# A graph network's head on one core: edge-list work moved in between the rows of the first table

## The chip, the core and the metric

The kernel runs on one core of a Trainium2 chip. The core has TensorE (PE in the profile; PEld is its weight load), VectorE (DVE), ScalarE (ACT), GpSimd (POOL) and SyncE (SP), which share an on-chip memory, SBUF, of 128 partitions; the large tables lie in the chip's DRAM and are moved by DMA. The metric is device time in microseconds, median of several runs.

## What is computed

Two layers on a graph of 12,500 nodes with 128 features and 212,500 edges, sorted by target node; an edge has a source, a target and one of nine types. Each layer normalises the rows, adds up the sources' rows for every target, and puts the sums through small dense layers:

```python
h = jnp.maximum(_layernorm(x, axis=-1), 0.0)
x = x + _L0_gnn_ref(h, edge_index, edge_type_9, 12500, ...)   # sum over edges of h[src] @ W_msg.T + emb[type], then a GRU cell
h = jnp.maximum(_layernorm(x, axis=-1), 0.0)
x = x + _L1_gnn_ref(h, edge_index, ...)                       # (1 + eps) * h + sum over edges, dense, batch norm, relu, dense
```

with `jax.ops.segment_sum(msg, dst, num_segments=num_nodes)` as the sum over edges in layer 0.

## The kernel before

**The head** (first 124 us of the profile) makes what layer 0 reads. It has two strands that share nothing but the engines.

The rows: x comes in 25 slices of up to 512 nodes (4 tiles of 128 rows). For each slice `normed` takes mean and variance on DVE (L426, L427), the root on ACT (L428), its reciprocal and the offset on DVE (L429, L430), and writes relu of the normalised rows on ACT (L434). `split0` cuts the fp32 rows into three bf16 parts, so that their sum is nearly exact: a cast on POOL (L444), a subtraction on DVE (L445), a cast (L446) and a subtraction (L447) on POOL. SP stores the three parts as rows of `table0` in DRAM (L208). `rows_ahead` has four buffers for the relu's result `h` and the three parts `hp0`. Eight slices of x are loaded at the start (L276), the others as their buffers come free.

The edge list: dst, src and type arrive as 128 by 1664 integers by nine DMAs issued on ACT (L268 to L273). DVE turns them into floats (L791, L793), adds nine to the type of an edge to itself (L796, L797), and packs the three into a word each (L814 to L817), which SP stores as `packed` (L818). PE and ACT turn dst, src and type into chunks of 128 edges (L806, L807). To find where each of 28 groups of 252 target nodes begins, DVE compares every 16th dst with the 28 group leads at once (L826) and adds up (L830); a matmul with ones sums over the partitions (L845), and `row_edge` (L853) says from which edge each row of the sort starts. L869 to L881 count the edges in front of the groups and look for lists that the fast way can't hold. The weights are loaded and turned by `first_weights` and what follows it (L411 to L416), with DMAs issued on POOL.

In the program's text the order is: lists' DMAs, x loads, constants, weights, list work, rows, checks of the lists. A planner orders each engine's instructions: of those whose inputs are there by its reckoning, the one that stands first in the text goes first. So it can fill gaps with later work. Each engine then runs its queue in order.

**The sort and the chunks.** From `in_order` (L1420) on, four engines keep the order of the text. One loop goes over 1064 chunks of 128 edges: for each chunk POOL gathers 128 rows of `table0` (L1218), DVE writes a 0/1 matrix of edge against node for eight chunks at a time (`m`, L1226), and PE multiplies (L1239, L1242). After each chunk the loop takes one step of `make_buckets`, which sorts the edges of the 28 groups by block of source nodes: it fetches the packed words with `row_edge` (L910), takes them apart on DVE (L948 to L971), then compares and swaps (L476) and turns (L599, L605). It also takes one step of `loading`, which puts `table0` into the SBUF table `held` in 24 DMAs (L1336, L1339); `held`'s end is cleared first (L1333). When the sort is through, this order ends, and the rest of layer 0 runs groups and chunks side by side under the planner again. Layer 1 repeats the scheme on the new rows.

**Memory.** Tiles that are no longer needed give their place to later ones, and the first instruction to touch a later tile waits for whoever used that place last. The head's tiles (`edges`, `xs`, `rows_ahead`) lie where later `cell`, `keys`, `matches0`, `held` and `buckets` lie.

Of the kernel before, what the change touches and what calls it, by code (L numbers as in the profile page):

```python
# [38 lines left out]
F32 = mybir.dt.float32  # L39
BF16 = mybir.dt.bfloat16  # L40
F32R = mybir.dt.float32r
I32 = mybir.dt.int32
AF = mybir.ActivationFunctionType
OP = mybir.AluOpType
AX = mybir.AxisListType
# [6 lines left out]
P = 128  # L52
SLICE = 512
BATCH = 8
BLOCK = 256
GROUP = 252
# [21 lines left out]
def tile_gnn(  # L78
# [175 lines left out]
    nodes0 = lists0.tile([P, QJ, QI, GROUPS - FIRST], BF16, name="nodes0")  # L254
    codes0 = lists0.tile([P, QJ, QI, GROUPS - FIRST], BF16, name="codes0")
# [9 lines left out]
    for name, v, pad in (("dst", dst, N), ("src", src, N), ("typ", edge_type, 0)):  # L265
        t = as_is[name] = epool.tile([P, ET, P], I32, name=f"{name}_is")
        nc.gpsimd.memset(t[:, full_t, :], pad)
        nc.scalar.dma_start(t[:, :full_t, :],  # L268
                            v[:full_t * P * P].rearrange("(t r e) -> r t e", r=P, e=P))
        r0 = full_t * P * P  # L270
        nc.scalar.dma_start(t[:rest_r, full_t, :],
                            v[r0:r0 + rest_r * P].rearrange("(r e) -> r e", e=P))
        nc.scalar.dma_start(t[rest_r:rest_r + 1, full_t, :rest_e],  # L273
                            v[r0 + rest_r * P:E].rearrange("(r e) -> r e", r=1))
    xpool = edges.enter_context(tc.tile_pool(name="xs", bufs=8))
    xs_of = {s: load_x(slices[s], xpool) for s in range(8)}  # L276
# [130 lines left out]
    def first_weights_done():  # L407
# [3 lines left out]
    first_weights(pool0)  # L411
    w_t = transposed((("1", w1), ("2", w2)), weights)
    b1_t, gamma_t, beta_t = (column(weights, v, n) for v, n in
                             ((b1, "b1_t"), (gamma, "gamma_t"), (beta, "beta_t")))
    b2_t = spread(weights, b2, P, "b2_t")
    eps1 = spread(weights, eps, P, "eps1")  # L416

# [20 lines left out]
    def split0(h, sl, cast, engine):  # L438

        m, p = len(sl.tiles), sl.high  # L440
        hp = env.rows.tile([P, PER, W0], BF16, name="hp0")
        part = [hp[:p, :m, k * D:(k + 1) * D] for k in range(PARTS0)]
        h = h[:p, :m, :]
        cast(part[0], h)  # L444
        nc.vector.tensor_tensor(h, h, part[0], op=OP.subtract)  # L445
        cast(part[1], h)  # L446
        engine.tensor_tensor(part[2], h, part[1], op=OP.subtract)  # L447
        return hp
# [339 lines left out]
    as_f = {}  # L788
    for name in ("dst", "src"):
        t = as_f[name] = epool.tile([P, ET, P], F32, name=f"{name}_f")  # L790
        nc.vector.tensor_copy(t, as_is[name])  # L791
    typ_f = as_f["typ"] = epool.tile([P, ET, P], F32, name="typ_f")
    nc.vector.tensor_scalar(typ_f, as_is["typ"], 0.0, float(NTYPES - 1), op0=OP.max, op1=OP.min)  # L793
    nc.vector.tensor_copy(as_is["typ"], typ_f)
    to_self = epool.tile([P, ET, P], F32, name="to_self")
    nc.vector.tensor_tensor(to_self, as_f["dst"], as_f["src"], op=OP.is_equal)  # L796
    nc.vector.scalar_tensor_tensor(typ_f, to_self, float(NTYPES), typ_f, op0=OP.mult, op1=OP.add)  # L797
    for b in range(0, ET, 4):
        k = min(4, ET - b)
        for name, t in (("dst", nodes), ("src", idx0), ("typ", code0)):  # L800
            some = min(k * P, t.shape[1] - b * P)
            if some <= 0:
                continue
            ps = turnp.tile([P, 4, P], F32, name="work")
            for j in range(some // P):
                nc.tensor.transpose(ps[:, j, :], as_f[name][:, b + j, :], ident)  # L806
            nc.scalar.copy(t[:, b * P:b * P + some], ps.rearrange("p k r -> p (k r)")[:, :some])  # L807
    to_f = epool.tile([P, cols0], F32, name="to_f")
    nc.vector.tensor_tensor(to_f, nodes[:, :cols0], start0, op=OP.subtract)
    nc.vector.tensor_scalar(to0, to_f, -1.0, float(BLOCK - 1), op0=OP.max, op1=OP.min)  # L810


    word = as_is["src"]
    nc.vector.tensor_single_scalar(word, word, 18, op=OP.logical_shift_left)  # L814
    nc.vector.tensor_single_scalar(as_is["dst"], as_is["dst"], 4, op=OP.logical_shift_left)
    nc.vector.tensor_tensor(word, word, as_is["dst"], op=OP.bitwise_or)
    nc.vector.tensor_tensor(word, word, as_is["typ"], op=OP.bitwise_or)  # L817
    nc.sync.dma_start(packed[:ET * P * P].rearrange("(t r e) -> r t e", r=P, e=P), word)  # L818
    tail = epool.tile([P, GE // P], I32, name="tail")
    nc.vector.memset(tail, N << 4)  # L820
    nc.sync.dma_start(packed[ET * P * P:].rearrange("(p c) -> p c", p=P), tail)

    samples = ET * P // SAMPLE
    leads = iota(epool, [P, GROUPS], [[GROUP, GROUPS]], base=SPLIT, name="leads")
    before = epool.tile([P, GROUPS, samples], BF16, name="before")
    nc.vector.tensor_tensor(  # L826
        before, as_f["dst"].rearrange("p t e -> p (t e)")[:, None, ::SAMPLE].to_broadcast([P, GROUPS, samples]),
        leads[:, :, None].to_broadcast([P, GROUPS, samples]), op=OP.is_lt)
    sampled = epool.tile([P, GROUPS], F32, name="sampled")
    nc.vector.tensor_reduce(sampled, before, axis=AX.X, op=OP.add)  # L830
    spread_sampled = epool.tile([P, 2, P], F32, name="spread_sampled")
    nc.vector.memset(spread_sampled, 0.0)
    for h in range(2):
        nc.vector.tensor_copy(spread_sampled[:, h, :GP].rearrange("p (g r) -> p g r", r=GROUP_ROWS),
                              sampled[:, :, None].to_broadcast([P, GROUPS, GROUP_ROWS]))
        nc.vector.tensor_copy(spread_sampled[:, h, GP:GP + GROUPS // 2], sampled[:, h::2])

    ps = turnp.tile([P, 4, P], F32, name="work")  # L840
    row_edge = lists0.tile([P, 2], I32, name="row_edge")
    first_edge = epool.tile([P, 2], F32, name="first_edge")
    in_group = epool.tile([P, 2], F32, name="in_group")
    for h in range(2):
        nc.tensor.matmul(ps[:, 0, h:h + 1], spread_sampled[:, h, :], ones, start=True, stop=True)  # L845

        here = in_group[:, h:h + 1]
        nc.vector.tensor_scalar(here, part_row[:, 0:1], float(-HALF), float(GROUP_ROWS * HALF - h * REST),
                                op0=OP.mult, op1=OP.add)
        nc.vector.scalar_tensor_tensor(here, here, behind, here, op0=OP.mult, op1=OP.subtract)  # L850
        nc.vector.tensor_scalar(here, here, float(GROUP_ROWS * HALF), None, op0=OP.add)
    nc.vector.tensor_scalar(first_edge, ps[:, 0, 0:2], -1.0, 0.0, op0=OP.add, op1=OP.max)
    nc.vector.scalar_tensor_tensor(row_edge, first_edge, float(SAMPLE), in_group, op0=OP.mult, op1=OP.add)  # L853

    layer_rows, env.rows = env.rows, edges.enter_context(tc.tile_pool(name="rows_ahead", bufs=4))
    for s, sl in enumerate(slices):
        xs = xs_of[s] if s in xs_of else load_x(sl, xpool)
        hp = split0(normed(sl, xs), sl, nc.gpsimd.tensor_copy, nc.gpsimd)
        rows_dma(table0, hp, sl, True)
    env.rows = layer_rows  # L860
    first_weights_done()
    nc.vector.tensor_scalar(eps1, eps1, 1.0, None, op0=OP.add)


    sent = epool.tile([P, 1], F32, name="sent")
    hit = epool.tile([P, ET * P], BF16, name="hit")
    bound = epool.tile([P, 1], F32, name="bound")
    nc.vector.memset(bound, 0.5 - SPLIT)
    nc.scalar.activation(hit, nodes, AF.Sign, bias=bound, accum_out=sent)  # L869
    totals = lists0.tile([1, 1], F32, name="totals")  # L870
    column_sums(totals, sent, -0.5, ET * P * P / 2)

    ends = stat.tile([P, 3], F32, name="ends")
    nc.vector.tensor_reduce(ends[:, 0:1], to_f[:, :CH0], axis=AX.X, op=OP.min)
    nc.vector.scalar_tensor_tensor(to_f, nodes[:, :cols0], float(SPLIT0), to_f, op0=OP.is_lt, op1=OP.mult)
    nc.vector.tensor_reduce(ends[:, 1:2], to_f[:, :CH0], axis=AX.X, op=OP.max)
    nc.vector.tensor_reduce(ends[:, 2:3], nodes[:, CH0:ALL], axis=AX.X, op=OP.min)
    nc.vector.tensor_scalar(ends[:, 0:1], ends[:, 0:1], -1.0, None, op0=OP.mult)
    nc.vector.tensor_scalar(ends[:, 1:2], ends[:, 1:2], float(1 - first_chunks.window), None, op0=OP.add)
    nc.vector.tensor_scalar(ends[:, 2:3], ends[:, 2:3], -1.0, float(SPLIT0), op0=OP.mult, op1=OP.add)  # L880
    worst_of(excess[:, 0:1], ends)  # L881
# [923 lines left out]
```

## Time and profile before

| | us |
|---|---|
| median of 3 runs (2593.80 to 2598.58) | 2594.92 |
| the profiled execution, all | 2603.78 |
| its span, first to last instruction | 2602.0 |
| head: to the first instruction of the sort on DVE (L948) | 124.02 |
| first gather of the table's rows on POOL (L1218) | 123.36 |
| busy in the span: PE, DVE, POOL, ACT | 2250.3, 2117.8, 1860.4, 1322.5 |
| busy from 0 to 124 us: PE, DVE, ACT, POOL | 13.73, 102.70, 57.19, 81.13 |

A line of a profile's group reads: line of the kernel, engine, operation, output<-input by the program's names, shape and type, number of instructions | busy us in all, mean ns of one | idle us of the engine just ahead of them, and what ended that idle time. A line of the timeline reads: start, length (of a merged run of the same instruction), engine, line, operation, names, number, and in brackets the idle time ahead of it with its releaser.

### The profile page before, as it was taken

To read this page: it belongs to the slowest core of one execution; us is meant where nothing else is said; L and a number is where in the kernel's file an instruction comes from. 1 tells how busy PE (TensorE), PEld (TensorE's weight loads), DVE (VectorE), ACT (ScalarE), POOL (GpSimd) and SP (SyncE) were. 2 spreads that over 40 slices of the span, in tenths; PEclk is the share of its full clock that TensorE was granted. 3 is DMA by queue.
4 is the path that set the end of the run, shared out by engine and by line. 5 is a ranking of instruction groups with operands and counts; after the bars stand their busy time and mean duration, and the time that the engine had idled before them with its cause. 6 is when DMAs were issued, how large, how long until landed. Compare 5 with 4: busy or idle time off the path is not lost. (4 is left out here: it accounts for less than half of the span.)

```text
span 2602.0 us, 52858 instructions
## 1 busy us (share of the span) xinstructions
PE 2250.3 (86%) x19810; PEld 1896.3 (73%) x19834; DVE 2117.8 (81%) x3899; ACT 1322.5 (51%) x2726; POOL 1860.4 (71%) x1886
## 2 busy tenths in 40 slices
PE   2033469899999999999999797899999999999996
PEld 1023347677677777777777575799999999999995
DVE  8898759896568878788787565699999999999983
ACT  4475125455566655656565364444444444444443
POOL 4876477777777777777777676377777777777770
PEclk9996659999999999999999898899999999999998
DMA  5662234454445444545455356655555555555584
GB/s 155 203 205 67 84 100 128 122 128 127 131 132 143 131 134 127 149 129 132 127 150 131 90 144 187 171 154 156 157 158 159 159 159 156 159 160 160 153 217 128
DMA packets 308267, 374.73 MB, mean 144 GB/s; under 512 B 44815, under 2 KB 263093, under 8 KB 308001
## 3 DMA queue, kind: packets, MB, share of 16 engines
q0 software_dynamic: 85504, 197.27, 28.7%
q1 hardware_dynamic: 217451, 171.44, 23.3%
q8 instruction: 158, 2.59, 0.4%
q10 hardware_dynamic: 5046, 2.55, 0.3%
q14 instruction: 108, 0.88, 0.1%
HBM read 327.18 MB, written 43.91 MB: 143 GB/s over the span
## 5 line engine op out<-in xcount | busy, mean ns | idle before, releaser
L1218 POOL DMA_INDIRECT g<-table,idx x1064 | 1070.9, 1006 | 354.9 <-issue 298.4
L1218 POOL DMA_INDIRECT g<-front,idx x690 | 692.8, 1004 | 258.5 <-issue 189.5
L1239 PE MATMUL bank<-m,g 128*128 128x128 bf16 (+25 forms) x5790 | 687.8, 232 | 101.5 <-DMA g<-table,idx 53.0
L1379 ACT CAST rows<-bank 128x384 bf16<-128x384 f32 x936 | 441.8, 478 | 410.3 <-PE bank L1377 407.6
L1542 ACT CAST rows<-bank 128x512 fp32r<-128x512 f32 x686 | 402.7, 588 | 470.8 <-PE bank L1539 468.3
L1539 PE MATMUL bank<-mine,take 126*128 126x256 f32 x2744 | 475.0, 295 | 16.0 <-issue 11.6
L1377 PE MATMUL bank<-held,take 128*128 128x384 bf16 x1872 | 464.5, 328 | 2.4 <-ACT rows L1379 1.6
L1386 PE MATMUL bank<-put,rows 128*128 128x252 bf16 x2808 | 460.1, 272 | 0.0
L1239 PEld LDWEIGHTS <-g 128*128 128x128 bf16 x3912 | 299.5, 103 | 200.0 <-DMA g<-table,idx 94.5
L1552 PE MATMUL bank<-put,rows 128*128 128x256 f32 x2744 | 443.1, 284 | 2.2 <-DVE put L1527 1.9
L1527 DVE TENSOR_TENSOR put<-places,nodes 128x1024 fp32r<-128x1024 f32 x343 | 412.9, 1213 | 5.4 <-PE bank L1552 5.4
L1358 DVE TENSOR_TENSOR put<-places,nodes 128x1008 bf16<-128x1008 f32 x234 | 281.3, 1202 | 157.0 <-PE bank L1388 156.7
L1539 PEld LDWEIGHTS bank<-mine,take 126*128 126x128 f32 x2744 | 374.2, 191 | 28.0 <-issue 21.8
L1552 PEld LDWEIGHTS bank<-put,rows 128*128 128x128 f32 x2744 | 378.0, 190 | 6.8 <-issue 3.6
L1386 PEld LDWEIGHTS <-rows 128*128 128x128 bf16 x2808 | 274.9, 98 | 130.1 <-issue 4.1
L1522 DVE TENSOR_SCALAR take<-others,own_row 126x512 fp32r<-126x512 bf16 x686 | 302.4, 491 | 64.1 <-PE bank L1539 33.6
L1226 DVE TENSOR_TENSOR m<-places,to 128x1024 bf16<-128x1024 f32 (+1 forms) x220 | 312.4, 1420 | 20.3 <-PE bank L1242 11.9
L476 DVE TENSOR_TENSOR key<-key 128x512 f32<-128x512 f32 (+1 forms) x470 | 297.2, 666 | 12.0 <-ACT key L607 4.0
L1239 PEld LDWEIGHTS bank<-m,g 128*128 128x128 f32 x1878 | 270.9, 190 | 2.7 <-DMA g<-front,idx 1.6
L1242 PE MATMUL bank<-m,kindsc 128*128 128x128 bf16 (+2 forms) x1304 | 269.9, 218 | 0.0
L1388 PE MATMUL bank<-put,kindsb 128*128 128x252 bf16 x936 | 254.4, 272 | 0.0
L1369 DVE TENSOR_SCALAR take<-others,own_row 128x512 bf16<-128x512 bf16 x468 | 151.6, 360 | 38.9 <-PE bank L1377 38.4
(329 smaller groups left out, 2189.7 us busy)
## 6 DMA issues: line engine op xcount, KB each, us to landing
others<-sources SPq DMA_DIRECT2D x343, 126.0 KB
others<-sources SPq DMA_DIRECT2D x234, 128.0 KB
g<-table,idx POOLq DMA_INDIRECT x1064
g<-front,idx POOLq DMA_INDIRECT x690
xs<-in_x_dram SPq DMA_DIRECT2D x39, 256.0 KB
table<-hp SPq DMA_DIRECT2D x24, 384.0 KB
held<-table SPq DMA_DIRECT2D x24, 384.0 KB
mine<-back SPq DMA_DIRECT2D x28, 252.0 KB
```

Of the source, the lines that this page charges most:

```text
L476: nc.vector.tensor_tensor(o, a, b, op=op)
L1218: nc.gpsimd.indirect_dma_start(out=into if table is table0 else into.bitcast(F32), out_offset=None, in_=table, in_offset=bass.IndirectOffs ...
L1226: nc.vector.tensor_tensor(m[:, :n, :], places[:, None, :w].to_broadcast([P, n, w]), to[:, c0:c0 + n, None].to_broadcast([P, n, w]), op=OP. ...
L1239: nc.tensor.matmul(tiles[0][:, lo:hi], g[:, j * D:(j + 1) * D], mk, start=False, stop=final and j == parts - 1, skip_group_check=True)
L1377: nc.tensor.matmul(ps, take[:, t, :], held[:, t0 + t, :], start=t == 0, stop=t == 1)
L1379: nc.scalar.copy(rows_, ps)
L1386: nc.tensor.matmul(sums[:, :GROUP], rows_[:, j * D:(j + 1) * D], put, start=False, stop=final and j == PARTS0 - 1, skip_group_check=True)
L1522: nc.vector.tensor_scalar(take[:GT, t, :n * P], others[:GT, :n * P], own_row[:GT, t:t + 1], None, op0=OP.is_equal)
L1527: nc.vector.tensor_tensor(put[:, :n, :], places[:, None, :].to_broadcast([P, n, BLOCK]), nodes1[:, j, q:q + n, None].to_broadcast([P, n, B ...
L1539: nc.tensor.matmul(ps[:, k, :], take[:GT, t, :], mine[bucket[1]][:GT, t, :], start=t == 0, stop=t == 1)
L1542: nc.scalar.copy(rows_, ps)
L1552: nc.tensor.matmul(to[:, c:c + BLOCK], rows_[:, k, j * D:(j + 1) * D], put, start=False, stop=final and j == PARTS - 1, skip_group_check=True)
```

## The change

The list's nine DMAs are issued on SP, between the loads of the first eight slices of x. The list work becomes a generator, `listed_edges`, of which each slice of rows but the first takes two steps, so that it stands between the slices in the text. The group leads are no longer compared in one instruction on DVE: ACT takes 28 Sign passes over every 16th dst, each with its sum. `split0` makes its first cast on ACT. The words of the sort are fetched in the head, into the place that the sort's result (`nodes0`, `codes0`, now one tile) takes later. The weights' loading moves behind the fifth slice. `rows_ahead` has six buffers. `held`'s end is cleared after its 24 loads.

```diff
-    nodes0 = lists0.tile([P, QJ, QI, GROUPS - FIRST], BF16, name="nodes0")
-    codes0 = lists0.tile([P, QJ, QI, GROUPS - FIRST], BF16, name="codes0")
+    both0 = lists0.tile([P, 2, QJ * QI * (GROUPS - FIRST)], BF16, name="both0")
+    nodes0, codes0 = (both0[:, k, :].rearrange("p (j i g) -> p j i g", j=QJ, i=QI) for k in range(2))
+    raw0 = both0.bitcast(I32).rearrange("p k n -> p (k n)")[:, :HALF]
...
-        nc.scalar.dma_start(t[:, :full_t, :],
+        nc.sync.dma_start(t[:, :full_t, :],
...
-    xs_of = {s: load_x(slices[s], xpool) for s in range(8)}
+    xs_of = {}
+    for s in range(8):
+        xs_of[s] = load_x(slices[s], xpool)
+        if s in (1, 3, 5):
+            load_edges(*(("dst", dst, N), ("src", src, N), ("typ", edge_type, 0))[s // 2])
...
-        cast(part[0], h)
+        nc.scalar.copy(part[0], h)
         nc.vector.tensor_tensor(h, h, part[0], op=OP.subtract)
-        cast(part[1], h)
-        engine.tensor_tensor(part[2], h, part[1], op=OP.subtract)
+        nc.gpsimd.tensor_copy(part[1], h)
+        nc.gpsimd.tensor_tensor(part[2], h, part[1], op=OP.subtract)
...
+    def listed_edges():
...
+        leads = iota(epool, [P, GROUPS], [[-GROUP, GROUPS]], base=-SPLIT, name="leads")
+        nc.vector.tensor_scalar(leads, leads, 0.5, None, op0=OP.add)
+        signs = epool.tile([P, samples], BF16, name="signs")
+        for g in range(GROUPS):
+            nc.scalar.activation(signs, as_f["dst"].rearrange("p t e -> p (t e)")[:, ::SAMPLE], AF.Sign,
+                                 bias=leads[:, g:g + 1], accum_out=sampled[:, g:g + 1])
+            if g % 4 == 3:
+                yield
...
-    before = epool.tile([P, GROUPS, samples], BF16, name="before")
-    nc.vector.tensor_tensor(
-        before, as_f["dst"].rearrange("p t e -> p (t e)")[:, None, ::SAMPLE].to_broadcast([P, GROUPS, samples]),
-        leads[:, :, None].to_broadcast([P, GROUPS, samples]), op=OP.is_lt)
-    sampled = epool.tile([P, GROUPS], F32, name="sampled")
-    nc.vector.tensor_reduce(sampled, before, axis=AX.X, op=OP.add)
...
+        for h in range(2):
+            nc.gpsimd.indirect_dma_start(
+                out=raw0[:, h * REST:(h + 1) * REST], out_offset=None,
+                in_=packed.rearrange("(e one) -> e one", one=1),
+                in_offset=bass.IndirectOffsetOnAxis(ap=row_edge[:, h:h + 1], axis=0))
...
-    layer_rows, env.rows = env.rows, edges.enter_context(tc.tile_pool(name="rows_ahead", bufs=4))
+    listed_ = listed_edges()
+    layer_rows, env.rows = env.rows, edges.enter_context(tc.tile_pool(name="rows_ahead", bufs=6))
     for s, sl in enumerate(slices):
         xs = xs_of[s] if s in xs_of else load_x(sl, xpool)
-        hp = split0(normed(sl, xs), sl, nc.gpsimd.tensor_copy, nc.gpsimd)
+        hp = split0(normed(sl, xs), sl)
         rows_dma(table0, hp, sl, True)
+        for _ in range(2 if s else 0):
+            next(listed_, None)
+        if s == 4:
+            first_weights(pool0)
...
+    for _ in listed_:
+        pass
...
     def make_buckets(keys, pool, psum):
-        raw = keys.tile([P, HALF], I32, name="key")
-        for h in range(2):
-            nc.gpsimd.indirect_dma_start(
...
-        nc.vector.memset(held[:, full:, :], 0.0)
-
         def loading():
-            nc.sync.dma_start(held[:N - full * P, full, :], table0[full * P:N, :])
             for t in range(0, full, 4):
...
                 yield
+            nc.vector.memset(held[:, full:, :], 0.0)
+            nc.sync.dma_start(held[:N - full * P, full, :], table0[full * P:N, :])
```

The steps of `listed_edges` that are not shown are the old instructions in this order: casts of dst and src, the Sign passes, the type, the packing and its store, `row_edge`, the fetch of the words, the edges to themselves, the turned chunks, the checks.

## The prediction

> **What bounds the kernel now.** I read the page's slices first: the first two (130 us) are the only ones in which TensorE (PE) is nearly idle while VectorE (DVE) works, and the diff moves instructions there alone. So I cut that head into stages with the view of busy time by window, then read its groups of instructions, then its end in the timeline. By window (columns: stretch, length, busy us and count for PE, PEld, DVE, ACT, POOL, granted clock, DMA share, GB/s):
>
> ```profile
> core 0: us, PE busy (x) PEld busy (x) DVE busy (x) ACT busy (x) POOL busy (x), PEclk, DMA share, GB/s
> 0.00:4.50 4.50, 0.00 (x0) 0.00 (x0) 1.13 (x8) 0.00 (x0) 3.94 (x14) 1.00 0.48 143
> 4.50:20.00 15.50, 1.11 (x4) 0.71 (x4) 11.09 (x64) 1.78 (x4) 8.66 (x13) 1.00 1.07 293
> 20.00:43.00 23.00, 11.90 (x40) 7.29 (x40) 21.07 (x21) 11.29 (x27) 2.90 (x5) 1.00 0.15 45
> 43.00:119.20 76.20, 0.71 (x4) 0.26 (x4) 69.18 (x278) 44.11 (x121) 61.73 (x77) 1.00 0.65 190
> 119.20:124.00 4.80, 0.00 (x0) 0.00 (x0) 0.22 (x1) 0.00 (x0) 3.90 (x6) 1.00 0.67 182
> ```
>
> Four stages follow one another: loading (DMA full, ScalarE (ACT) empty), the edge lists (DVE full, POOL and DMA empty), the rows of the table (DVE 69.18 of 76.2, 91%; POOL 81%; ACT 58%), and 4.8 us in which DVE does nothing. DVE is the fullest throughout: 102.5 us busy of 119.2. The groups of 0 to 119.2 us, shapes kept apart (busy, mean ns | idle before):
>
> ```profile
> L434 ACT ACTIVATE h<-xs,nb,rs 128x128 f32<-128x128 f32 x98 | 39.1, 480 | 17.3 <-DVE nb L430 15.8 <-issue 0.9 <-DMA table<-hp 0.5
> L447 POOL TENSOR_TENSOR hp<-h,hp 128x512 bf16<-128x512 f32 x24 | 28.7, 1196 | 0.9
> L445 DVE TENSOR_TENSOR h<-h,hp 128x512 f32<-128x512 f32 x24 | 27.5, 1150 | 6.6 <-POOL hp L444 6.1
> ...
> L446 POOL CAST hp<-h 128x512 bf16<-128x512 f32 x24 | 16.3, 680 | 11.3 <-DVE h L445 8.3 <-DVE nb L430 3.1
> L444 POOL CAST hp<-h 128x512 bf16<-128x512 f32 x24 | 16.0, 670 | 19.7 <-ACT h L434 19.7
> ...
> L430 DVE SCALAR_TENSOR_TENSOR nb<-mv,rs 128x4 f32<-128x4 f32 x24 | 6.7, 294 | 0.0
> ...
> L826 DVE TENSOR_TENSOR before<-dst_f,leads 128x2912 bf16<-128x2912 f32 x1 | 5.1, 5067 | 0.0
> ...
> L830 DVE TENSOR_REDUCE sampled<-before 128x28 f32<-128x2912 bf16 x1 | 3.2, 3167 | 0.0
> ```
>
> L444 first starts at 45 us (its 19.7 us of idle): no row of the table is made earlier, because ACT's first instruction comes at 18.2 us, behind its nine DMA issues, and DVE then does the lists first. The timeline at the head's end:
>
> ```profile
> 118.98 0.17 DVE L934 MEMSET front<- 128x128 f32 x1
> ...
> 120.61 1.04 POOL L910 DMA_INDIRECT key<-packed,row_edge  x1 [0.16 <-issue]
> ...
> 122.88 0.22 DVE L1333 MEMSET held<- 128x192 uint32 x1 [3.74 <-DMA table<-hp]
> ...
> 123.36 0.95 POOL L1218 DMA_INDIRECT g<-table,idx  x1 [0.44 <-issue]
> ...
> 124.02 0.54 DVE L948 TENSOR_SCALAR ints<-key 128x512 int32<-128x512 int32 x1 [0.92 <-DMA key<-packed,row_edge]
> ```
>
> DVE waits 3.74 us in a memset for the last stores of the table and 0.92 us for the keys; only then does the sort (L948 on) begin. From there DVE sets the pace: in each 10 us from 140 to 220 it is busy 9.7 to 9.8, 16 compares (10.59 us) and one match per eight chunks, and PE waits for the match (3.93 us at 172, 5.29 at 184). Gathers have slack: PE is done with the first eight chunks at 138.7 us, and DVE needs their match buffer at 147.27. So what counts is when L948 starts: 124.0 now, with 2478.0 us behind it.
>
> **The change, part by part.** *DVE.* The comparison with all group leads and its reduction go: 5.07 + 3.17 = 8.24 us. Two small scalings come: some 0.15 us each by L310's row. 102.5 - 8.2 + 0.3 = 94.6 us. Inside that lies waiting that counts as busy: L445 takes 0.69 us where POOL runs nothing and 1.63 where it runs L447, on average 1.150; L430 takes 0.14 or up to 1.11, on average 0.294. That is 24 x 0.46 + 24 x 0.154 = 14.7 us blocked by POOL. Per slice POOL's 0.67 + 0.68 + 1.20 = 2.55 us lose the first cast: 26% less. I take 26% of 14.7, 3.9 us, off: 90.7 us. Bounds: half of it goes (87.3), or none goes and a dozen list operations, which had POOL idle beside them, each meet half a 1.2 us L447 (101.8).
>
> *ACT.* Off go nine DMA issues, which hold it until 18.2 us. On come 25 casts of 128x512 and 28 Sign passes over 104 samples. A cast costs 0.586 (L807, same size, from PSUM): 24.5 x 0.586 = 14.4 us. A Sign with its sum costs 0.717 for 512 elements (L981, start to start); elements cost 0.83 ns (L807: 0.586 against 0.267 for 128), so 104 cost some 0.38: 10.6 us, or 20 at L981's full price. ACT: 57.2 + 14.4 + 10.6 = 82.2 us (to 92), from 58% of the row stage to about 80%: no longer idle, still below DVE.
>
> *POOL.* Off go 16 us of casts. The weights' fifteen DMA issues (0.52 to 1.14 us, 10.2 in all, now at 4.8 to 24 us) come after the fifth slice, two waits for PE with them (3.55 and 4.86), and the key fetch (2.0 us) from 120.6 into the middle. POOL in the rows: 61.7 - 16 + 10.2 + 2 = 58 us. Behind a waiting key fetch (0.83 MB of packed list to land first, some 4 us at 190 GB/s) stand the next slices' casts; six row buffers times 3 us per slice hide 4 us and 8.4 of weights; with no cover they cost that once. L910's 2.0 us lay before the first gather but in the wait for the table: taking it away gives POOL nothing.
> The row here is 0.52 to 1.14 us per issue on POOL; the three from 13.3 to 16.2 us, beside a busy DVE, are 0.80, 1.14 and 0.91. A rule of the Trainium skill speaks against that move: "SBUF — State Buffer", section "A bandwidth-pool intuition that's wrong", has a DMA issued by POOL go from some 620 to 3100 ns beside a VectorE copy that holds the port the two share. By the page's figure (an estimate) fifteen issues would take 46 us, POOL 94, and at 91% the head would end at 108 us, a gain of 16.
>
> *SP.* Nine list DMAs (2.55 MB) go between the x loads: at 293 GB/s xs 6 and 7 land near 18 us, not 10, and the stores queue behind. Six slices need no store landed for 18 us, and DVE has constants, casts and five slices to do. Cover gone: the 3 us that DVE lost to loading now (11.09 of 15.5 against 91%). I keep 3, zero to 6 as bounds. The order of the reads is else indifferent: the DMA share is 0.15 at 20 to 43 us.
>
> *The end.* The memset of `held` moves behind the 24 loads, so DVE's 3.74 us of wait go; keys are there, so 0.92 go. 0.22 us are done later, on DVE: nothing.
>
> **The sum.** DVE: 4.5 us to the first x (1.1 of work in it) + (90.7 - 1.1) / 0.91 + 3 = 106 us, then L948 at once: 124 - 106 = 18 us. Table landed 3.7 us after DVE's end as now: gathers from 110, first eight chunks done at 125, match needed at 129: slack left. The profiled execution took 2603.78 us, span 2602.0, so 2584 of span and 2586 in all; the median of the runs shown is 2594.92, 8.9 below it, and 2594.9 - 18 = 2577. Ends: (87.3 - 1.1) / 0.97 + 4.5 = 93, a gain of 31; (101.8 - 1.1) / 0.90 + 4.5 + 6 = 122, a gain of 2.
>
> **The rivals.** *ACT becomes the bound, slower.* The chain of a slice goes DVE, ACT (root), DVE, ACT (relu, now cast), DVE, POOL; ACT serves its queue in order, and list copies and Signs stand between the relus. It decides from 69%: if ACT is busy less than 82.2 / (124 - 4.5), the head is longer than now. At 62% L948 starts at 137: +13, 2608. For it: ACT sat at 58% in the row stage with 15.8 us of waits for L430. Against: in those waits DVE, not ACT, was full, and from 146 to 220 ACT ran without a gap.
> *Same.* ACT at 69 to 72%, or ends in the list work that give back what is won: 2590 to 2598.
> *The early keys don't help.* Tiles of the sort lie where the head's buffers lay. By shape: head 116 KB per partition before, 121 after (comparison 5.8 less, two row buffers of 5 KB more); cell, keys, matches and `held` 118. So `lead` and `front`, free until now (`lead` ran at 109.9), come to lie under the top row buffer. If one of the last two slices owns it, DVE again waits for stores, then has 4.5 us of `lead` to `front` to do: L948 at 113, gain 11, 2584.
> *The later part is replanned.* Behind the hand-ordered part the planner orders; PE is busy 1155.96 of 1200 us there. One per cent is 12 us: 2589 with the gain, slower only with more.
>
> **How the numbers follow.** Forecast (gain 6 to 31) 0.72, early keys don't help 0.08, same 0.08, ACT bound or replanned for the worse 0.12. Some 0.2% (5 us) can be told from no change. Faster 0.80, same 0.08, slower 0.12. The range 2564 to 2594 covers the first two cases and part of the third, and leaves out the slower ones.
>
> **What would show it.** Right: ACT's first instruction by 6 us, not 18.2; first relu by 10, not 43.5; L446 alone of POOL's two casts left; L948's successor at 100 to 112 us with no wait for stores before it; ACT near 80% in the head; 2478 us, to 3, from there to the end. A later start of that instruction with DVE under 80% busy and ACT the releaser of its waits shows the first rival; a start in time with a longer rest shows the last. I am wrong if DVE is 90% busy and the head still ends after 118: then its work was not what I summed.

## The result, and the profile after

| | before | changed |
|---|---|---|
| median of 20 runs each, us | 2594.82 (2590.63 to 2601.65) | 2590.53 (2582.57 to 2597.36) |
| ratio, 95% interval | | 0.9979 (0.9970 to 0.9988) |
| four traces each, means: first integer step of the sort on DVE, us | 123.9 | 113.9 |
| first gather on POOL | 123.2 | 109.9 |
| last Sign of the sort on ACT | 220.7 | 210.1 |
| from there to the end | 2376.1 | 2378.8 |

The changed kernel is 4.3 us faster (3.1 to 7.8 by the interval); 18 were forecast. On two chips used later every run of every kernel, the one before too, took 3509 to 3692 us; from the traces taken there only the first 163 us are read, in which their clock is full. The profiled execution took 2597.36 us, span 2595.5. Line numbers move by 1 to 30: the first cast is now ACT L445, the integer steps of the sort begin at L976, the gathers at L1246.

The stages of the head, by window (columns as before the change):

```profile
core 0: us, PE busy (x) PEld busy (x) DVE busy (x) ACT busy (x) POOL busy (x), PEclk, DMA share, GB/s
4.50:20.00 15.50, 1.38 (x4) 0.68 (x4) 13.66 (x67) 6.32 (x17) 9.82 (x14) 1.00 1.03 302
20.00:43.00 23.00, 1.60 (x5) 0.86 (x5) 22.92 (x81) 22.56 (x83) 13.29 (x15) 1.00 0.76 224
43.00:60.00 17.00, 4.36 (x16) 3.07 (x16) 17.00 (x70) 11.99 (x36) 11.93 (x12) 1.00 0.54 171
80.00:100.00 20.00, 0.00 (x0) 0.00 (x0) 17.78 (x57) 19.16 (x49) 15.15 (x18) 1.00 0.56 182
...
0.00:103.50 103.50, 13.79 (x47) 8.19 (x47) 94.18 (x356) 81.69 (x232) 67.29 (x84) 1.00 0.66 201
103.50:113.20 9.70, 0.00 (x0) 0.00 (x0) 4.20 (x16) 0.00 (x0) 5.69 (x8) 1.00 0.68 213
```

The stage "lists alone" is gone: rows and lists share all of it, DVE is full from 20 to 60 us, and towards the end ACT (19.16 of 20) is the fuller one. The groups of 0 to 113 us, shapes apart:

```profile
L446 DVE TENSOR_TENSOR h<-h,hp 128x512 f32<-128x512 f32 x24 | 23.1, 963 | 2.6 <-ACT hp L445 1.8 <-POOL kindsb L1345 0.3
L447 POOL CAST hp<-h 128x512 bf16<-128x512 f32 x24 | 19.4, 810 | 32.2 <-DVE h L446 30.7 <-DVE first_edge L847 1.5
L445 ACT CAST hp<-h 128x512 bf16<-128x512 f32 x24 | 14.5, 605 | 0.0
L804 ACT ACTIVATE signs<-dst_f,leads 128x104 bf16<-128x104 f32 x28 | 12.9, 462 | 8.1 <-DVE leads L801 8.1
L431 DVE SCALAR_TENSOR_TENSOR nb<-mv,rs 128x4 f32<-128x4 f32 x24 | 8.2, 358 | 0.3
L804 ACT ACTIVATION_READ_ACCUMULATOR signs<-dst_f,leads 128x1 f32 x28 | 5.3, 188 | 0.0
```

One cast is left on POOL, and the subtraction on DVE fell from 1150 to 963 ns. A Sign takes 462 ns and the reading of its sum 188, but the two overlap each other and what follows; in the timeline of ACT the next instruction starts 0.47 us after the Sign:

```profile
23.07 0.47 ACT L804 ACTIVATE signs<-dst_f,leads 128x104 bf16<-128x104 f32 x1
...
23.54 0.60 ACT L445 CAST hp<-h 128x512 bf16<-128x512 f32 x1
```

Now the end of the head in the timeline:

```profile
101.40 2.02 DVE L446 TENSOR_TENSOR h<-h,hp 128x512 f32<-128x512 f32 x2
108.79 0.17 DVE L943 TENSOR_SCALAR lead<-own_group 128x2 f32<-128x2 f32 x1 [5.36 <-DMA table<-hp]
109.16 0.99 POOL L1246 DMA_INDIRECT g<-table,idx  x1 [2.94 <-DMA table<-hp]
113.09 0.17 DVE L962 MEMSET front<- 128x128 f32 x1
113.17 0.36 DVE L976 TENSOR_SCALAR ints<-both 128x512 int32<-128x512 int32 x1
```

DVE ends the rows at 103.43. The memset of `held` is gone from here, but `lead` now waits 5.36 us for the stores of the table, and behind it come 4.4 us of small steps (`lead` to `front`, two matches among them) that the kernel before did between 109.9 and 119.2 us, among its last rows and ahead of its wait. So the wait for the stores was not removed; it moved to another instruction.

### The profile page after: what moved, and what is told of

Its sections match the earlier page's. It is cut to its first block, busy times and chain, and to the rows that moved or that the text cites. A ratio compares the mean times of both kernels' runs of the same rounds, so it can differ in the third digit from the quotient of the medians.

```text
span 2595.5 us, 52944 instructions
## 1 busy us (share of the span) xinstructions
PE 2246.4 (87%) x19810; PEld 1894.9 (73%) x19834; DVE 2113.3 (81%) x3899; ACT 1347.0 (52%) x2807; POOL 1852.3 (71%) x1861
## 5 line engine op out<-in xcount | busy, mean ns | idle before, releaser
L1246 POOL DMA_INDIRECT g<-table,idx x1064 | 1075.8, 1011 | 362.3 <-issue 298.2
L1246 POOL DMA_INDIRECT g<-front,idx x690 | 690.6, 1001 | 254.1 <-issue 192.2
L1385 DVE TENSOR_TENSOR put<-places,both 128x1008 bf16<-128x1008 f32 x234 | 281.1, 1201 | 160.1 <-PE bank L1415 159.9
```

The source lines that it names most:

```text
L1246: nc.gpsimd.indirect_dma_start(out=into if table is table0 else into.bitcast(F32), out_offset=None, in_=table, in_offset=bass.IndirectOffs ...
```

## The experiments

A table of the heads first (us; means of four traces for the kernel before and the changed one; two traces where two numbers stand):

| kernel | DVE's last step on rows | first integer step | first gather | last Sign of the sort |
|---|---|---|---|---|
| before | 117.3 | 123.9 | 123.2 | 220.7 |
| changed | 104.2 | 113.9 | 109.9 | 210.1 |
| free_lead | 112.6 | 93.6 | 118.1 | 213.3 |
| five_rows | 112.9 | 93.9 | 118.4 | 213.6 |
| early_lead | 111.6 | 91.8 | 117.6 | 212.7 |
| late_sort | 104.9 | 130.9 | 110.6 | 227.3 |
| ordered_lead | 106.1 | 93.0 | 112.1 | 207.9 |
| behind_rows | 105.2, 104.3 | 111.2, 110.4 | 111.0, 110.1 | |
| early_behind | 105.8, 105.5 | 105.8, 105.5 | 112.1, 111.8 | |
| signs_dve | 115.3 | 123.5 | 119.4 | |
| cast_pool | 109.2 | 118.9 | 114.9 | |
| lists_act | 106.6 | 116.4 | 112.3 | |

The last five rows come from the two chips of which only the first 163 us are read.

**Does the loss repeat?** The two kernels unchanged, three more traces of each.

> The changed kernel once more, to see whether its loss behind the head repeats. Theory 'the loss is lawful': the head again ends 10.9 us earlier (first integer step of the sort at 113, before 124.0), the 800 gathers from number 160 to 960 again take 1059 to 1060 us (before: 1053.1), and the time is 4 to 5 us below before. Rival 'the loss is chance': the same head, but the stretch of gathers takes anything between 1052 and 1060 us, and the span differs from 2595.5 by several us.

> The kernel before once more, for the spread of its own trace. Theory 'the profiled execution of before was a long one': the head ends within 1 us of where it did (first integer step of the sort at 123 to 125, last Sign of the sort at 220 to 222), and the span is 2594 to 2596, 6 to 8 us below the 2602.0 of the first profile, lost behind the head by chance. Rival 'before's head varies': first integer step at 118 to 121.

> A third trace of the kernel before. Theory 'chance behind the head': last Sign of the sort at 220 to 221 again, and from there to the end 2372 to 2382 (2381.2 and 2374.3 in the first two). Rival 'the head varies': last Sign of the sort more than 1.5 off 220.6.

> A fourth trace of the kernel before, for the mean and spread of the same two stretches: last Sign of the sort at 220 to 221, then 2372 to 2382 to the end. If the mean of the four second stretches is under 2376, the changed kernel (2386.1 and 2379.1 so far) is slower behind the head; if it is 2377 to 2379, it is not.

> A third trace of the changed kernel. Theory 'chance behind the head': last Sign of the sort at 209 to 212, then 2372 to 2380 to the end, the kernel before's own 2378 on average. Rival 'lawful loss behind the head': 2380 or more from the last Sign to the end.

> A fourth trace of the changed kernel, for the mean and spread of the same two stretches. Theory 'chance': the head's gain is 9 to 11 in every trace and the second stretch agrees with that of the kernel before within 2 us on average. Rival 'lawful loss': the mean of the second stretch stays 4 us or more above that of the kernel before.

after_again: 2589.68 us against 2597.28, ratio 0.9969 (0.9953 to 0.9984). The single traces: 2596.62, 2599.66 and 2594.33 for the kernel before, 2585.31 and 2588.05 for the changed one. The stretch of 800 gathers that took 1059.7 us in the first trace of the changed kernel took 1053.5, 1053.3 and 1053.3 in the others, 1051.8 to 1056.2 in the kernel before: the loss there was chance. The last Sign of the sort is at 220.82, 220.50, 220.60, 220.74 before and 209.35, 211.34, 209.23, 210.50 after: the head's gain, 10.6 on average, repeats. From there to the end: 2381.2, 2374.3, 2377.2, 2371.8 before, 2386.1, 2379.1, 2374.3, 2375.8 after. The means differ by 2.7, with a standard deviation of 4 to 5 in each four, so this sum alone decides between neither theory; where it arises is taken up below.

**Take the wait for the stores away.** In three ways.

```diff
 free_lead (lead, tile_i, more and front in the place of nodes1, which is written only later)
+    room = nodes1.bitcast(F32).rearrange("p j g -> p (j g)")
...
-        lead = pool.tile([P, 2], F32, name="lead")
+        lead = small["lead"]
...
 five_rows
-    layer_rows, env.rows = env.rows, edges.enter_context(tc.tile_pool(name="rows_ahead", bufs=6))
+    layer_rows, env.rows = env.rows, edges.enter_context(tc.tile_pool(name="rows_ahead", bufs=5))
 early_lead (free_lead, and the steps from lead to front inside the loop over the slices)
+        if s == 15:
+            lead_tiles(**small)
```

> The four small tiles with which the sort begins (lead, tile_i, more, front) lie in nodes1, which is written only later, and so no longer under the top row buffer. Theory 'overlay': lead no longer waits for the stores (5.36 us in the changed kernel), it starts at 103.5 to 104.5, the first integer step at 108 to 109 instead of 113.2. Rival 'the stores are waited for anyway': first integer step stays at 113. For the end: if the sort's start is carried through, 4 to 5 us below the changed kernel (2586); if the gathers' stream bounds layer 0, whose first gather still waits for the table at 109, nothing (2590).

> Five row buffers instead of six: the highest ends at 207104 of a partition, below the sort's tiles (209664 on). Theory 'overlay': lead starts as soon as VectorE is through with the rows, first integer step 4.4 us behind that; with the rows themselves no slower than 1 us the first integer step comes at 108 to 110, and the time is that of free_lead. Rival 'the sixth buffer is needed': the rows end 2 us or more later than 103.4, because ScalarE and VectorE wait for stores, and the time is that of the changed kernel or worse.

> As free_lead, and the dozen small steps from lead to front (4.4 us in a row with nothing beside them) are done behind slice 15 of the table, where VectorE is busy 17.8 of 20 us. Theory 'VectorE has room there': first integer step at 104 to 106, 7 to 9 us before the changed kernel; 2582 if the sort's start is carried through, 2590 if the gathers' stream bounds layer 0. Rival 'the head has no room': the rows end 4 us later, first integer step at 108, as in free_lead.

Measured: 2593.49 (0.9981, 0.9971 to 0.9991), 2592.77 (0.9987, 0.9976 to 0.9998), 2595.32 (0.9992, 0.9982 to 1.0002), where the changed kernel, measured beside them, has 2589.68 (0.9969). All three took the wait away, began the sort 20 us earlier, and were no faster than the changed kernel. The timeline of DVE in five_rows says why:

```profile
106.25 0.69 DVE L989 TENSOR_TENSOR ints<-key 128x512 int32<-128x512 f32 x1
...
107.60 0.68 DVE L446 TENSOR_TENSOR h<-h,hp 128x512 f32<-128x512 f32 x1
108.20 0.68 DVE L992 SCALAR_TENSOR_TENSOR blocks<-bad,ints 128x512 f32<-128x512 bf16 x1
```

Steps of the sort (L989 to L992) stand between the last rows (L446). What the overlay (a tile that lies where an earlier one lay) had held back was free now, and the planner put it into the rows' gaps; the rows ended 7 to 9 us later, and with them the first gather (118). Then the early sort waits again, here in free_lead (the view of waits of DVE from 112 to 208 us):

```profile
DVE edge_of L1007 <- POOL edge_of L292: 12.6, 1, 12.6
```

`edge_of` is an iota on POOL that stands behind sixteen gathers in POOL's queue. With the gathers starting at 118.1 it comes at 138.38, and DVE needs it at 126. So the sort is tied to the first gather as well: the last Sign came 95.1 to 95.2 us after it in these three. In the changed kernel the iota runs at 130.17 and is needed at 134.63: 4.3 us of slack.

**Which sets the end, the sort's start or the gathers?** The sort is delayed alone (64 memsets, which took 16.44 us and not 10.9).

```diff
 late_sort
-        nc.vector.memset(front, 0.0)
+        for _ in range(64):
+            nc.vector.memset(front, 0.0)
```

> 64 memsets of front (0.17 us each, 10.9 us) instead of one, ahead of the sort's first integer step: the sort starts 10.7 us later, at 124, as in the kernel before, and the table and the first gather (109) stay early. Theory 'the sort's start sets the end': last Sign of the sort at 220, time 2600 (2590 and 10.7). Rival 'the gathers' stream sets it': most of the delay is hidden, time 2591 to 2594.

First integer step 130.9, last Sign 227.3 (17.2 later), first gather 110.6; 2605.68 us, ratio 1.0038 (1.0024 to 1.0051), that is 15 to 18 us above the changed kernel by the ratios (0.9979 and 0.9969). The sort's start is carried to the end almost one to one; gathers that start early hide nothing of it.

**Take the wait away and keep the rows first.**

```diff
 ordered_lead (early_lead, and)
+    nc.vector.scalar_tensor_tensor(small["lead"], hp[:, 0, :2], 0.0, small["lead"], op0=OP.mult, op1=OP.add)
 behind_rows (free_lead, and the steps from lead to front and the integer steps queued behind the last L446)
+        with tc.issue_after(last_row):
+            nc.vector.tensor_scalar(lead, own_group, float(GROUP), float(SPLIT), op0=OP.mult, op1=OP.add)
 early_behind (early_lead, and only the integer steps queued behind the last L446)
```

> As early_lead, but the last step of lead also reads the last slice's finished row (times zero), so that the sort's integer steps can't be put between the last rows as they were in free_lead, five_rows and early_lead. Theory 'the sort's start sets the end, and mixing it with the rows was what cost': rows end at 104 to 106 and the table's first gather comes at 110 to 112, the sort's second step at 105 to 107 against 113.5 in the changed kernel, last Sign of the sort at 202 to 205; time 2582 to 2585. Rival 'the gathers' stream sets it': the same head, time 2590.

> The small tiles lie in nodes1 as in free_lead, but VectorE's steps from lead to the first integer steps are queued behind its last step on the rows, so that its order is that of the changed kernel and only the wait for the stores is gone. Theory 'the overlay's wait is part of the missing gain': rows end at 103.5, lead right behind, first integer step at 108 instead of 113.2, first gather unchanged at 109 to 111, last Sign of the sort at 204 to 205.5 instead of 210.1, time 5 us below the changed kernel (2585 where before has 2596). Rival 'the sort then waits for something else, or runs slower beside the stores': last Sign of the sort at 208 or later, time 2588 to 2591.

> As early_lead, with the integer steps queued behind VectorE's last step on the rows: the steps from lead to front and the first two matches are done among the rows (4.4 us), the integer steps come right behind them. Theory 'VectorE has room among the rows': rows end at 104 to 105, first integer step there, last Sign of the sort at 200 to 202, time 8 to 9 us below the changed kernel (2581 to 2582 where before has 2596). Rival 'no room': rows end at 107 to 108, last Sign at 204 to 205, time as behind_rows, and the first gather 4 us later than there.

> behind_rows once more. Theory 'the sort's start is carried to the end': first integer step at 107 to 109, last Sign of the sort 96.2 later (203 to 205), 2377 us from there, time 2582 to 2584 where before has 2596 (ratio 0.995). Rival 'something else takes it': last Sign as early, but time 2588 to 2591 (ratio 0.9975), as the changed kernel.

> early_behind once more. Theory 'the sort's start is carried to the end': first integer step at 105, last Sign of the sort at 201 to 202, time 2580 to 2582 (ratio 0.994). Rival 'the first gather, 2 to 3 us later than in the changed kernel, or something else takes it': time 2586 to 2590.

ordered_lead: 2587.96 against 2595.93, ratio 0.9974 (0.9964 to 0.9984), as fast as the changed kernel. Its step with `lead` (106.6) comes 8.6 us before the changed kernel's (115.2), but the last Sign only 2.2: DVE comes to `edge_of` earlier and waits 5.0 us for it there, as the gathers ahead of the iota start no earlier but 2.2 us later. The end of the rows in behind_rows_2:

```profile
102.30 2.02 DVE L450 TENSOR_TENSOR h<-h,hp 128x512 f32<-128x512 f32 x2
104.24 0.57 DVE L951 TENSOR_SCALAR nodes<-own_group 128x2 f32<-128x2 f32 x1
...
110.36 0.37 DVE L983 TENSOR_SCALAR ints<-both 128x512 int32<-128x512 int32 x1
```

`lead` (here in `nodes`) follows the last row at once: the wait was the overlay's, as DVE's order in the head is the changed kernel's and only the place of the tiles differs. Of its 5.3 us 3.1 are won (first integer step 110.8 on average against 113.9): the small steps now run beside POOL's last casts and take 6.1 us in place of 4.4, and the rows ended 0.6 later. In early_behind the integer steps start right behind the rows, 8.3 us before the changed kernel's, with the first gather 2 us later. The times can't say what these starts are worth: ratios 0.9997 (0.9967 to 1.0026) and 0.9982 (0.9943 to 1.0021), on the second of those chips 0.9968 (0.9940 to 0.9997) and 0.9969 (0.9943 to 0.9995). That stays open.

**Which terms of the forecast's sum were right?** Single parts undone.

```diff
 signs_dve (as before the change: one comparison and a reduction on DVE)
-        for g in range(GROUPS):
-            nc.scalar.activation(signs, as_f["dst"].rearrange("p t e -> p (t e)")[:, ::SAMPLE], AF.Sign,
-                                 bias=leads[:, g:g + 1], accum_out=sampled[:, g:g + 1])
...
+        nc.vector.tensor_tensor(
+            before, as_f["dst"].rearrange("p t e -> p (t e)")[:, None, ::SAMPLE].to_broadcast([P, GROUPS, samples]),
+            leads[:, :, None].to_broadcast([P, GROUPS, samples]), op=OP.is_lt)
...
+        nc.vector.tensor_reduce(sampled, before, axis=AX.X, op=OP.add)
 cast_pool
-        nc.scalar.copy(part[0], h)
+        nc.gpsimd.tensor_copy(part[0], h)
 lists_act
-        nc.sync.dma_start(t[:, :full_t, :],
+        nc.scalar.dma_start(t[:, :full_t, :],
```

> The comparison with all group leads and its reduction are back on VectorE (5.07 and 3.17 us in the kernel before), the 28 Signs leave ScalarE; all else as in the changed kernel. Theory of the forecast 'VectorE is the bound': the rows end 8 us later, last Sign of the sort at 218, time 2598. Rival 'ScalarE is the bound there (22.56 busy of 23 us from 20 to 43, 28 Signs at 0.65 us are 18 us of it)': the rows end no later than 103 to 105, last Sign at 208 to 211, time 2588 to 2591.

> The first of the row's casts goes back from ScalarE to GpSimd, which then has 0.67 and 0.68 and 1.20 us per slice again; all else as in the changed kernel. Theory of the forecast 'the cast's move relieves VectorE by 3.9 us': rows end 4 us later, last Sign of the sort at 214, time 2594. Rival 'ScalarE is the bound from 77 to 103 us (2.45 us per slice, 0.60 of it the cast)': rows end 2 to 5 us earlier, last Sign at 205 to 208, time 2585 to 2588.

> The nine loads of the edge list are issued by ScalarE again, at the same places in the text; all else as in the changed kernel. Theory of the forecast 'the loads held ScalarE until 18.2 us, and its first relu is worth what VectorE loses without it': ScalarE's first relu at 12 us or later instead of 6.1, rows end 2 to 6 us later than 104, time 2 to 6 us above the changed kernel (2592 to 2596). Rival 'VectorE has the lists to do meanwhile, so it is no loss': rows end within 1 us of 104, time as the changed kernel (2590).

The rows end 11.1, 5.0 and 2.4 us later than the changed kernel's 104.2. In signs_dve the comparison took 6.31 and the reduction 3.17 us, together 9.5. In cast_pool the 5.0 are as large as expected but come another way: not the subtraction grew (893 ns, 963 in the changed kernel), DVE waited for POOL's cast.

```profile
L446 DVE TENSOR_TENSOR h<-h,hp 128x512 f32<-128x512 f32 x24 | 21.4, 893 | 13.6 <-POOL hp L445 13.5
```

In lists_act ACT's first relu comes at 20.1 in place of 6.1 and costs only 2.4, because DVE has the lists to do meanwhile (busy 11.29 us from 4.5 to 20, 13.66 in the changed kernel). The three add up to 18.5, more than the 13.1 by which the whole change ended the rows earlier (117.3 to 104.2): they share some of the same time. Their ratios, 1.0027 (0.9994 to 1.0059), 0.9989 (0.9952 to 1.0026) and 0.9962 (0.9933 to 0.9991), come from those two chips and are too wide to rank them.

**Where the rest goes.** Behind the head the changed kernel's engines run the old instructions in the old order, but for the memset of `held`, which the change moves. So the nth instruction from the end can be set beside the nth. Counted from the last Sign of the sort, ACT's instructions of the changed kernel stand no more than 1.7 us from those of the kernel before between 400 and 1400 us, 0.6 between 1500 and 2320, and 2.5 to 3.2 later from 2320 on (means of four each; the single traces of a kernel scatter there by some 3 to 4 us, as a standard deviation). The jump lies at one wait, the last take of a list block in layer 1. The DMA issues on SP and DVE's wait in the kernel before (before_again):

```profile
2527.41 3.34 SPq L210 DMA_DIRECT2D mine<-resid  x4
2530.86 3.20 SPq L1518 DMA_DIRECT2D others<-sources  x1
2540.37 0.88 DVE L1522 TENSOR_SCALAR take<-others,own_row 126x512 fp32r<-126x512 bf16 x2 [4.19 <-DMA others<-sources]
2540.91 1.02 PE L1539 MATMUL bank<-mine,take 126*128 126x256 f32 x4 [2.09 <-DVE take L1522]
```

and in the changed kernel (after_c):

```profile
2512.79 4.34 SPq L210 DMA_DIRECT2D mine<-resid  x4
2517.24 2.91 SPq L1545 DMA_DIRECT2D others<-sources  x1
2528.77 0.88 DVE L1549 TENSOR_SCALAR take<-others,own_row 126x512 fp32r<-126x512 bf16 x2 [6.92 <-DMA others<-sources]
2529.31 1.41 PE L1566 MATMUL bank<-mine,take 126*128 126x256 f32 x4 [5.23 <-DVE take L1549]
```

The last load of `others` stands behind four loads of `mine`, whose issue takes SP 2.43, 3.34, 2.75 and 2.91 us in the four traces before, and 6.82, 5.37, 4.34 and 5.50 after; PE's gap ahead of the matmul that waits for that take is 2.72, 2.09, 2.92, 1.72 before and 4.42, 4.78, 5.23, 4.81 after, 2.4 us more on average. So that much of the head's gain is lost 2300 us later. The slow issue alone does not make the gap: in free_lead, five_rows, early_lead and ordered_lead the same four loads take SP 5.31 to 7.44 us, and PE's gap there is 1.55 to 2.67 (late_sort: 5.28 and 4.48). No instruction there was changed, and the cause stays open.

## Why the prediction was right or wrong

Right in direction, and 2590.5 lies in the range, but the gain is a quarter of the forecast's 18 (7.6 us in the second set of runs, after_again). In the head 10.0 of the 18 came; 5.3 went into a wait that the forecast had struck out, 2.6 into a DVE sum that was too small.

- *The DVE sum.* It put the end of all of DVE's work in the head at 106, the steps from `lead` to `front` included, as they lie in its 102.5. The rows ended at 104.2 on average, and with 4.4 us for these steps that makes 108.6 without the wait: 2.6 late, and so near partly by luck. DVE was busy 98.4 us in all (94.18 and 4.20 by the windows above), not 90.7. The 8.2 for the comparison hold (signs_dve). The subtraction fell by 4.5 us, where 3.9 were forecast for less blocking by POOL, but L431 rose by 1.5, and list work that now runs beside POOL costs more: the cast of src 2.04 instead of 1.03, one of the "two small scalings" (L801) 1.52 instead of 0.15. The forecast had this only in its bound of 101.8. Nor does cast_pool confirm the term, for its 5.0 are waiting and not blocking. In return DVE idled less: without the wait it was busy 93% from 4.5 us on, where the sum had 88% (91% and 3 us for loading; up to 20 us it was busy 13.66 of 15.5, before 11.09).
- *ACT.* The cast was right (0.586 forecast, 0.605), a Sign a little too cheap: 0.38 forecast, 0.46 measured from its start to the next instruction (0.58 if that is another Sign), some 13 us and not 10.6. The 18 us in the expectation of signs_dve add up durations that overlap. ACT was busy 81.69 us of the first 103.5, 79%, as forecast (82.2, 80%), so the first rival, for which it had to be under 69%, did not come. ACT is the fuller engine at the end, but cast_pool and signs_dve, which relieve it at the cost of POOL and DVE, both end later.
- *POOL.* The eighteen loads that POOL issues in the head took 12.0 us, 11.9 before, 0.48 to 1.35 us each; the 46 us of the estimate by the page's figure were far off. The rule of the Trainium skill ("SBUF — State Buffer", section "A bandwidth-pool intuition that's wrong") shows all the same: it has an issue that meets a VectorE copy wait until some 115 ns after that instruction's end. In the changed kernel:

```profile
24.74 1.35 POOL L393 DMA_DIRECT2D beta_t<-in_L_gnn_beta_dram  x1
24.99 0.99 DVE L810 CAST typ_is<-typ_f 128x1664 int32<-128x1664 f32 x1
```

  The issue ends some 0.12 us behind the cast (25.98). All seven issues over 0.85 us in the four traces of the changed kernel end 0.12 us behind a DVE cast or scaling of 1664 elements. So the page's 3100 ns is no price for every issue beside a busy DVE: one or two of the eighteen waited, each no longer than one instruction of 1.0 to 1.4 us.
- *The step that failed: "then L948 at once".* The sum let the sort begin where DVE's work ends, at 106. It began at 113.9 on average: 2.6 us by the sum above, and 5.3 of wait for the table's stores in `lead`, which the sum had at nothing. This is the rival "the early keys don't help", nearly with its figures (L948 at 113, gain 11), to which 0.08 was given. What pointed to it was there: six buffers in place of four, 121 KB of head against 118 KB of later tiles in the rival's own count, and the stores' wait that already stood in the memset of `held`. A wait that was taken from one instruction was forecast as gone; the next instruction to touch that memory had it. behind_rows shows that it is the place of the tiles; free_lead shows that taking the wait away and leaving the order to the planner gains nothing (0.9981 beside the changed kernel's 0.9969).
- *"2478.0 us behind it unchanged."* From the first integer step to the end it was 2472.9 before and 2475.0 after, on four traces each (the forecast's 2478.0 is the longest of the four before). late_sort shows that a shift of the sort is carried to the end; some 2.4 us are lost in the wait for the last `others`. The head's 10.6 less the 2.7 of the rest are the 7.9 by which the mean spans of the four traces differ (2596.8 and 2588.9); the medians of the larger sets say 4.3 and 7.6.
- *"From there DVE sets the pace."* In the 60 us up to the last Sign ACT is busy 60.00 us and DVE 58.8, before and after the change. From `edge_of` on DVE to the last Sign it takes 74.7 to 74.9 us in all thirteen traces that are read beyond the head, 104 Signs at 0.72 us: from there ACT sets the pace. That is why a later `edge_of` moves the end of the sort one to one.
- *"Gathers have slack".* It was counted at the match buffer. The nearer tie is `edge_of`: 4.3 us of slack in the changed kernel, whose sort starts at 113.9. In early_behind, whose sort starts at 105.6, DVE waits 3.7 to 3.8 us there in both traces. So the forecast's 18 could not have been had without an earlier table as well.
- The planner rival is refuted: the order behind the head is the same on all engines, the memset of `held` apart.

## What to carry to other kernels

When a change takes a wait off one instruction, ask which later instruction is the next to touch the same memory, and price the gain from there. Work that a wait holds back is not free to run when the wait goes: a planner may put it ahead of what everything else needs. And when a strand starts earlier, look on every engine's queue for small things it needs (here one iota behind sixteen gathers). Moving that iota into the head, with behind_rows, was not tried.

## What the runs showed of the hardware

- In the 60 us up to the last Sign of the sort the granted clock was 0.61 and 0.69 in two traces of the changed kernel (after_c, after_d) and 0.61 in late_sort, 0.87 in before_again and ordered_lead. From its first integer step to that Sign the sort took 96.2 us in all four traces of the changed kernel, 96.4 in late_sort, 96.8 in the kernel before: in this stage, where ACT is full, the time does not follow TensorE's clock. The stretches at half rate last 3.4 us or a multiple of that (6.8, 10.2, 30.7, up to 85.3), the last of a trace apart; the Trainium skill ("TensorE: Matmul & The Clock Gate", "Part 1: The HAM clock gate (the "warmup" mystery)") names a window of 3413 ns, and the traces agree.
- In the first comparison the twenty runs of each kernel spread by 11 and 15 us, and the stretch behind the head by 9 and 12 in four traces each. A difference of 4 us is not to be read from a pair of traces, but from medians of many runs, or from stretches that repeat to 0.3 us, such as the kernel before's head.
